# One edge addition instead of two in layer 2, and a blocked layout with one normalization in layer 3

## The chip, the cores and the metric

The kernel runs on one core of a Trainium2 chip, as one launch. The metric is the device time in microseconds of one execution, from the first to the last instruction and the little that lies around them. The numbers are fp32 throughout.

## The reference

Four residual layers follow each other on an image batch of 16 x 64 channels x 128 x 128. Each first normalizes over groups of two channels. Layer 0 multiplies by the image's Gram matrix and a 64 x 64 matrix, layer 1 is a pair of 3 x 3 Scharr-like filters per channel, layer 2 shifts a quarter of the channels one column to the left and a quarter to the right and then has a 3 x 3 convolution with bias, layer 3 has a 3 x 3 convolution, a 1 x 1 convolution and a normalization over the whole batch.

```python
def _gn(v, G=32, eps=1e-5):                       # before every layer
    g = v.reshape(B_, G, C_ // G, H_, W_)
    m = jnp.mean(g, axis=(2, 3, 4), keepdims=True)
    s = jnp.var(g, axis=(2, 3, 4), keepdims=True)
    return ((g - m) / jnp.sqrt(s + eps)).reshape(v.shape)

def _L2_conv_ref(x, W, b):
    def _temporal_shift(x):
        q = x.shape[1] // 4
        left = jnp.concatenate([x[:, :q, :, 1:], jnp.zeros_like(x[:, :q, :, :1])], axis=-1)
        right = jnp.concatenate([jnp.zeros_like(x[:, q:2 * q, :, :1]), x[:, q:2 * q, :, :-1]], axis=-1)
        return jnp.concatenate([left, right, x[:, 2 * q:]], axis=1)
    xs = _temporal_shift(x)
    out = lax.conv_general_dilated(xs, W, window_strides=(1, 1), padding='SAME', ...)
    return out + b[None, :, None, None]

def _L3_conv_ref(x, w_bin, w1x1, b1x1, gamma, beta):
    y = _conv(x, w_bin, [(1, 1), (1, 1)])
    y = _conv(y, w1x1, [(0, 0), (0, 0)]) + b1x1[None, :, None, None]
    mean = jnp.mean(y, axis=(0, 2, 3), keepdims=True)
    var = jnp.var(y, axis=(0, 2, 3), keepdims=True)
    y = (y - mean) * jax.lax.rsqrt(var + EPS)
    y = y * gamma[None, :, None, None] + beta[None, :, None, None]
    y = jnp.where(y >= 0, y, LEAK * y)
    return jnp.clip(y, 0.0, CEIL)

x = x + _L0_conv_ref(_gn(x), L0_conv_conv_w)
x = x + _L1_conv_ref(_gn(x))
x = x + _L2_conv_ref(_gn(x), L2_conv_W, L2_conv_b)
x = x + _L3_conv_ref(_gn(x), L3_conv_w_bin, L3_conv_w1x1, L3_conv_b1x1, L3_conv_gamma, L3_conv_beta)
```

## The kernel before

**Tiling.** Two halves of 64 fill the 128 partitions: for layers 0 and 1 the upper and the lower half of the rows of an image, for layers 2 and 3 two parities of rows. An image is worked in `NS = 8` chunks; a chunk is `R = 8` rows of 128 columns for each partition (`CP = 4` rows of each parity).

**Stages and their order.** Four stages work on different images at the same time: `Gram` (the image's Gram matrix and the small chain of coefficients behind it), `Front` (layers 0 and 1, called the front below), `Layer2` and `Layer3`. The main loop (lines 1055 to 1111) runs over steps, each of four quarters `q`. In each quarter Layer 3 comes first, then Layer 2, then Front, then Gram; they start 35, 25 and 15 steps in, and 8 steps further for every image. So in one step, one chunk of each of three images is worked. All engines' instructions keep the order in which the program issues them (the class `InOrder`); there is no scheduler that moves them. A matmul is issued for the two column halves of the array in turn, from two queues (`held`, `issue`, lines 721 to 741).

**Layer 2.** `load` (line 773) fetches the chunk `i + 2`, `at(i, 1)` normalizes the chunk `i + 1` on ACT in place (line 867), lets POOL compute the `edges` of it (lines 870 to 877: for each of the end columns, 8 rows, a term which the shift of the reference needs there), and POOL clears the end columns of the shifted quarters. A row convolution of three rows is split as in a fast algorithm: one product on the odd rows that two outputs share (`one`), and products on differences of rows (`d2`, made by DVE in `difference`, line 703) that belong to one output row each (`two[:, 0]`, `two[:, 1]`). A twin `qd2` of each difference, with half of it shifted by a column, is written by two DMAs that POOL issues (`twin`, line 808). Products start in `at(i, 2)` and `at(i, 3)`. `one` is evicted to `c` by ACT. One step later, in `at(i, 0)` (lines 838 to 850), DVE adds the edges to the end columns of `two`, side by side in two operations:

```python
e = self.edges.pop(i - 1).rearrange("p t (m n) -> p t n m", n=2)
for side, w in ((0, 0), (1, W - 1)):
    dve.tensor_add(two[:, :, :, w], two[:, :, :, w], e[:, side])
```

and then forms the chunk `x3` = `two` + `c`, with the sums for the next normalization. `x3` has its rows in two blocks, `[2, CP, W]`; ACT squares and sums it (`square`), and SP stores it for the end. When an image is through, `coefficients` (line 308) makes the scale and bias of layer 3 by a chain of small operations on DVE, PE and ACT, and the sums of layer 2's input do the same for the front's next image.

**Layer 3.** `prepare(i + 1)` in `at(i, 1)` (lines 928 to 946) writes the normalized chunk to the tile `v3`, two buffers of `R + 1 = 9` rows, in the order of the image: row 0 is the last of the chunk before, the odd rows 1, 3, 5, 7 are the first block of `x3`, the rows 2, 4, 6, 8 its second. This takes three activations on ACT: of one row, of four rows with a step of two, and of four rows with a step of two. The last chunk of an image needs a fourth, as its last row takes other coefficients. `by_parity` (line 699) gives the even and odd rows as views, `difference` reads even, odd, and the even ones one further (`after`), and `shared` gives the odd ones to the matmuls. `twin` here is two copies on ACT (line 948). The sum `y` = `two` + `c` is stored by SP; its mean and square sums gather over the whole batch.

**The end.** Once all images are through, the batch's coefficients are made (lines 1115 to 1138), and a last pass reads `y` and `x3` back by DMA in 128 parts, has ACT and DVE finish them, and stores the output. The room for prefetched parts comes from tiles that are done (`rest`, line 1033), among them the two `v3` buffers, of which 8 rows are used.

Of the kernel before, what the change touches and what calls it, by code (L numbers as in the profile page):

```python
# [10 lines left out]
F32 = mybir.dt.float32  # L11
# [4 lines left out]
B, C, H, W = 16, 64, 128, 128  # L16
P = 128
# [3 lines left out]
R = 8  # L21
NS = HH // R
EARLY = 3
CP = 4
# [84 lines left out]
def tile_kernel(ctx: ExitStack, tc: tile.TileContext, x, cw_h, w2_t, b2, wbin_t, w1_t, b1, gamma, beta, consts, out):  # L109
    nc = tc.nc  # L110
    pe, dve, act, sp, pool = (InOrder(tc, e) for e in (nc.tensor, nc.vector, nc.scalar, nc.sync, nc.gpsimd))
# [8 lines left out]
    def k(name):  # L120
        return kc[:, AT[name][0]:AT[name][1]]
# [14 lines left out]
    def flat(ap):  # L136
        return ap.rearrange("p j w -> p (j w)")
# [17 lines left out]
    ring = ctx.enter_context(tc.tile_pool(name="ring", bufs=2))  # L155
# [35 lines left out]

    wb = ring.tile([P, (R + 1) * W + 2], F32, tag="v2", name="wb", bufs=3)
    wb = wb[0:C, 0:9 * C].rearrange("p (y x c) -> p y x c", y=3, x=3)
    w1 = ring.tile([P, R + 1, W], F32, tag="v3", name="w1")[0:C, 0, 0:C]

    sp.dma_start(kc[:, 0:P], consts[:, 0:P])
    pool.dma_start(kc[:, P:K_END], consts[:, P:K_END])
# [499 lines left out]


    def by_parity(t):
        v = t[:, 0:R, :].rearrange("p (j s) w -> p s j w", s=2)  # L700
        return v[:, 0], v[:, 1]

    def difference(name, n, t, m=CP):


        even, odd = by_parity(t)
        after = t[:, 1:R + 1, :].rearrange("p (j s) w -> p s j w", s=2)[:, 1]
        dve.tensor_sub(diffs[name][:, n, 0:m, 1:1 + W], (after if n else even)[:, 0:m], odd[:, 0:m])

    def taps(o, p, wts, srcs, pad=0):  # L710
# [37 lines left out]
    def shared(p, wt, t, m=CP):  # L748
        products(p[:, 0:m], [wt], [by_parity(t)[1][:, 0:m]])
# [15 lines left out]
    class Layer2:  # L765
# [65 lines left out]
        def at(self, i, q):  # L831
            b = self.b
            closing = i + 1 == NS
            m = CP - 1 if closing else CP
            if q == 0:
                if i == NS:
                    chains.append(coefficients(self.st, self.done))
                if 1 <= i:
                    two = self.p.pop(i - 1)[0]

                    e = self.edges.pop(i - 1).rearrange("p t (m n) -> p t n m", n=2)
                    for side, w in ((0, 0), (1, W - 1)):
                        dve.tensor_add(two[:, :, :, w], two[:, :, :, w], e[:, side])
                    x3 = ring.tile([P, 2, CP, W], F32, tag="x3", name=f"x3_{b}_{i - 1}", bufs=NS + 2)
                    tiles3[b].append(x3)
                    dve.scalar_tensor_tensor(
                        x3.rearrange("p s j w -> p s (j w)"), two.rearrange("p s j w -> p s (j w)"), 1.0,
                        self.c.unsqueeze(1).to_broadcast([P, 2, CP * W]),
                        op0=ALU.mult, op1=ALU.add, accum_out=self.st[:, 0, i - 1:i],
                    )  # L850
                if 0 <= i < NS:
                    difference("d2", 0, self.v[i], m)
                    self.twin(0)
            if q == 1:
                if i == 0:

                    self.wi = stp.tile([P, 2, 3, P], F32, tag="wi", name=f"wi_{b}", bufs=1)
                    for n, base in ((0, w2[:, 2]), (1, wm)):
                        dve.scalar_tensor_tensor(
                            self.wi[:, n].rearrange("p k o -> p (k o)"), k("I3"), self.co[:, 2:3],  # L860
                            base.rearrange("p k o -> p (k o)"), op0=ALU.mult, op1=ALU.add,
                        )
                if -1 <= i < NS - 1:
                    if i == -1:
                        self.co = coefs2.pop(b)
                    t, f = self.v[i + 1], self.whole.pop(i + 1)
                    act.activation(f, f, AF.Identity, bias=self.co[:, 1:2], scale=self.co[:, 0:1])


                    e = stp.tile([P, 2, R], F32, tag="edges", name=f"edges_{b}_{i + 1}", bufs=3)  # L870
                    for side, at in ((0, 0), (1, W + 1)):
                        for rows, j in ((lo, 1), (hi, 0)):
                            n = at + j * W
                            pool.tensor_scalar_mul(
                                e[rows, side], f[rows, n:n + (R - 1) * W + 1:W], self.co[rows, 3 + side:4 + side]
                            )
                    self.edges[i + 1] = e

                    pool.tensor_scalar_mul(t[:, :, 0], t[:, :, 0], k("keep0"))
                    pool.tensor_scalar_mul(t[:, :, W - 1], t[:, :, W - 1], k("keep1"))  # L880
                if i + 2 < NS:
                    self.load(i + 2)
            if q == 2:
                if 0 <= i < NS:
                    t = self.v[i]
                    one = ps_one.tile([P, CP, W], F32, tag="one", name=f"one2_{b}_{i}")
                    two = ps_two.tile([P, 2, CP, W], F32, tag="two", name=f"two2_{b}_{i}")
                    self.p[i] = two, one
                    shared(one, self.wi[:, 0], t, m)
                    if closing:  # L890
                        small_product(one[:, m, :], w0, t[:, R, :])

                    both = self.wi[:, 1]
                    own(two[:, 1], 1, TO_SLOTS, w2, "d2", m, both)
                    if closing:

                        p = two[:, 1, m:CP]
                        issue([taps(0, p, [both], [t[:, R:R + 1, :]]), taps(1, p, [both], [t[:, R - 1:R, :]])])

                    self.c = ring.tile([P, CP * W], F32, tag="c2", name=f"c2_{b}_{i}", bufs=1)  # L900
                    act.activation(self.c, flat(one), AF.Identity, bias=self.co[:, 5:6])
                if 1 <= i < NS:
                    self.square(i - 1)
                if 1 <= i:
                    self.store(i - 1)
            if q == 3:
                if 0 <= i < NS:
                    t = self.v.pop(i)
                    two, one = self.p[i]
                    both = self.wi[:, 1]  # L910
                    own(two[:, 0], 0, TO_SLOTS, w2, "d2", m, both)
                    if closing:
                        p, srcs = two[:, 0, m:CP], [t[:, R - 2:R - 1, :], t[:, R - 1:R, :]]
                        issue([taps(0, p, [w2[:, 0], both], srcs), taps(1, p, [both, w2[:, 1]], srcs)])
            if q == "last of 0" and i == NS:
                self.square(i - 1)
            if q == "last of 3" and -1 <= i < NS - 1:
                difference("d2", 1, self.v[i + 1], CP if i + 2 < NS else CP - 1)
                self.twin(1)


    class Layer3:
# [4 lines left out]

        def prepare(self, i):
            b, tiles = self.b, tiles3[self.b]
            t = ring.tile([P, R + 1, W], F32, tag="v3", name=f"v3_{b}_{i}")  # L930
            self.v[i] = t

            def norm(dst, src, co):
                act.activation(dst, src, AF.Identity, bias=co[:, 1:2], scale=co[:, 0:1])

            if i == 0:
                self.co, self.edge = coefs3.pop(b)
                norm(t[:, 0, :], tiles[NS - 1][:, 1, CP - 1, :], self.edge["lower"])
            else:
                norm(t[:, 0, :], tiles[i - 1][:, 1, CP - 1, :], self.co)  # L940
            v = t[:, 1:R + 1, :].rearrange("p (n s) w -> p s n w", s=2)
            norm(v[:, 0], tiles[i][:, 0], self.co)
            m = CP if i + 1 < NS else CP - 1
            norm(v[:, 1, 0:m], tiles[i][:, 1, 0:m], self.co)
            if m < CP:
                norm(t[:, R, :], tiles[i][:, 1, m, :], self.edge["upper"])

        def twin(self, n):

# [83 lines left out]
    def rest(pool, tag, shape, bufs, n=None):  # L1033
        for m in range(bufs if n is None else n):
            t = pool.tile([P] + shape, F32, tag=tag, name=f"end_{tag}_{len(room)}", bufs=bufs)
            while len(t.shape) > 2:
                t = t.rearrange("p a b c -> p (a b) c" if len(t.shape) == 4 else "p a b -> p (a b)")
            room.append(t[:, 0:N])
# [16 lines left out]
    for step in range(starts[2][1] - 2, steps):  # L1055
        now[0] = step
        for q in range(4):
            for b in range(B):

                i = step - starts[2][1] - NS * b  # L1060
# [10 lines left out]
            for b in range(1, B):  # L1071
                at, n = pace[b]
# [25 lines left out]
            if step >= last_one and q == 2:  # L1098

                n = 3 if step == last_one else 1 if step < last_one + NS - 2 else 0  # L1100
# [5 lines left out]
        tick()  # L1106
    rest(ring, "x3", [2, CP, W], NS + 2, NS + 2 - 3 - (NS - 3))
    rest(ring, "y", [2, CP, W], 2)
    rest(ring, "v3", [R + 1, W], 2)
    while len(room) > 1:  # L1110
        fetch()

# [17 lines left out]
    e = cpool.tile([P, 1], F32, name="e_bn")  # L1130
# [56 lines left out]
```

## Time and profile before

| | us |
|---|---|
| median of 3 runs | 2742.17 |
| lowest and highest | 2739.24 and 2742.29 |
| the profiled execution, its own time | 2739.81 |
| span of the profiled execution | 2738.0 |
| busy: PE | 2168.3 (79%) |
| busy: DVE | 2190.3 (80%) |
| busy: ACT | 2108.3 (77%) |
| busy: POOL | 851.7 (31%) |
| mean granted clock of PE, whole span | 0.899 |

PE is the matmul engine (PEld its weight loads, which overlap matmuls), DVE the vector engine, ACT the scalar engine, POOL GpSimd, SP the engine that issues most of the DMAs. A group of instructions is given by line, engine, operation, names of the tiles written and read with partitions x elements, and count; then busy time, mean duration in ns, and the idle time of the engine before them with what ended it. All groups have line 73, as every operation goes through the helper there; so one goes by the tiles' names. In the names, buffer numbers are left out: `two<-two,edges` is the edge addition, `v<-x,co` layer 3's normalization, `v<-v,co` layer 2's, `d<-v` a difference, `qd<-d` a twin.

The page has the span in 40 slices of 68 us. The main loop takes about the first 2290 us; PE, DVE and ACT are at 90% or near it from slice 6 to slice 29. Layer 3 of the last image runs alone just before 2290, and from there on the DMAs move 420 GB/s.

### The profile page before, as it was taken

How to read it: one execution, taken by the hardware profiler on the slowest of the kernel's cores; microseconds unless marked ns; L12 is line 12 of the kernel's file. 1: busy time of each engine (PE TensorE's matmuls, PEld its weight loads, DVE VectorE, ACT ScalarE, POOL GpSimd, SP SyncE). 2: the span in 40 equal slices, each digit the busy share in tenths (PEclk: the TensorE clock that was granted, in tenths of full speed). 3: DMA queues.
4: the chain of work that ended last, by engine and by line, in shares of the span. 5: the costliest groups of instructions: out<-in, count | busy, mean ns of one | idle time of the engine just before them, and what ended most of it. 6: DMA issues, size and time to landing. Idle time of an engine off the chain costs nothing. (4 is left out here: it accounts for less than half of the span.)

```text
span 2738.0 us, 45982 instructions
## 1 busy us (share of the span) xinstructions
PE 2168.3 (79%) x14804; PEld 910.8 (33%) x14804; DVE 2190.3 (80%) x3623; ACT 2108.3 (77%) x3177; POOL 851.7 (31%) x1350
## 2 busy tenths in 40 slices
PE   6578899999999999999999999999999993000000
PEld 4234433434343434343434343333334641000000
DVE  4999999999999999999999999999996335333332
ACT  4766889898989898989899989898997677333332
POOL 2044424442434243333343434445444300000000
PEclk8689999999999999999999999999999997555555
DMA  8799878898888888888889787888887868999999
GB/s 209 200 232 235 224 198 238 217 240 220 236 231 234 226 228 226 228 224 234 224 226 239 211 201 201 204 211 207 220 204 187 226 188 308 419 420 420 420 420 385
DMA packets 693600, 685.95 MB, mean 251 GB/s; under 512 B 60096, under 2 KB 580448, under 8 KB 693360
## 3 DMA queue, kind: packets, MB, share of 16 engines
q1 hardware_dynamic: 668208, 613.83, 76.2%
q0 software_dynamic: 25152, 69.18, 10.0%
q8 instruction: 119, 1.95, 0.3%
q14 instruction: 121, 0.99, 0.1%
HBM read 346.23 MB, written 268.44 MB: 224 GB/s over the span
## 5 line engine op out<-in xcount | busy, mean ns | idle before, releaser
L73 PE MATMUL two<-d,w 128*64 128x508 f32 (+2 forms) x2560 | 855.5, 587 | 0.0
L73 PE MATMUL two<-d,wi 128*64 128x508 f32 (+3 forms) x1536 | 576.1, 578 | 0.0
L73 PE MATMUL two<-qd,pk 128*64 128x512 f32 (+1 forms) x1024 | 521.0, 590 | 27.9 <-DMA qd<-d 19.8
L73 POOL DMA_DIRECT2D qd<-d x512 | 270.8, 531 | 862.4 <-DVE d L73 284.5
L73 POOL TENSOR_SCALAR edges<-v,co 64x8 f32<-64x8 f32 x512 | 334.9, 654 | 352.5 <-ACT v L73 183.8
L73 DVE TENSOR_TENSOR d<-v 128x512 f32<-128x512 f32 (+1 forms) x512 | 346.0, 678 | 58.1 <-issue 30.8
L73 PEld LDWEIGHTS two<-d,w 128*64 128x64 f32 x2560 | 273.0, 136 | 325.1 <-issue 282.1
L73 PE MATMUL one<-v,w 128*64 128x508 f32 (+2 forms) x1600 | 364.6, 579 | 0.0
L73 PE MATMUL one<-v,wi 128*64 128x508 f32 (+3 forms) x1536 | 353.3, 591 | 2.5 <-issue 1.7
L73 ACT COPY qd<-d 64x512 f32<-64x512 f32 x512 | 315.5, 616 | 18.2 <-DVE d L73 12.2
L73 DVE SCALAR_TENSOR_TENSOR e<-e 128x1032 f32<-128x1032 f32 (+1 forms) x256 | 313.0, 1223 | 0.0
L73 ACT ACTIVATE xh<-po,co 128x128 f32<-128x128 f32 (+1 forms) x480 | 275.4, 623 | 26.1 <-PE po L73 22.4
L73 PEld LDWEIGHTS two<-d,wi 128*64 128x64 f32 x1536 | 178.8, 136 | 200.6 <-issue 178.8
L73 ACT ACTIVATE v<-x,co 128x512 f32<-128x512 f32 (+2 forms) x368 | 235.0, 705 | 0.0
L73 DVE SCALAR_TENSOR_TENSOR y<-two,c 128x1024 f32<-128x1024 f32 x128 | 156.0, 1219 | 94.6 <-ACT v L73 72.6
L73 POOL TENSOR_SCALAR v<-v,kc 128x9 f32<-128x9 f32 x256 | 217.9, 864 | 11.9
L73 PE MATMUL po<-x,abd 64*64 64x512 f32 (+1 forms) x1024 | 177.7, 640 | 46.5 <-ACT xh L73 43.1
L73 ACT ACTIVATE u<-u 128x1024 f32<-128x1024 f32 x128 | 135.4, 1058 | 75.1 <-DVE u L73 74.7
L73 PEld LDWEIGHTS two<-qd,pk 128*64 128x64 f32 x1024 | 130.8, 135 | 183.1 <-issue 86.4
L73 PEld LDWEIGHTS one<-v,w 128*64 128x64 f32 x1600 | 132.1, 136 | 171.7 <-issue 142.8
L73 DVE SCALAR_TENSOR_TENSOR u<-xh 128x1170 f32<-128x1170 f32 x128 | 175.4, 1370 | 3.8 <-ACT xh L73 3.8
L73 ACT ACTIVATE v<-v,co 128x1154 f32<-128x1154 f32 x128 | 172.1, 1345 | 6.0 <-DMA x_d<-x 3.3
(165 smaller groups left out, 3259.1 us busy)
## 6 DMA issues: line engine op xcount, KB each, us to landing
x<-in_x SPq DMA_DIRECT2D x256, 256.0 KB, 4.6
x_d<-u SPq DMA_DIRECT2D x512, 128.0 KB, 4.0
y_d<-y SPq DMA_DIRECT2D x512, 128.0 KB, 3.9
x_d<-x SPq DMA_DIRECT2D x496, 128.0 KB, 2.7
xr<-in_x SPq DMA_DIRECT2D x120, 512.0 KB, 6.2
qd<-d POOLq DMA_DIRECT2D x256, 130.0 KB, 3.4
qd<-d POOLq DMA_DIRECT2D x256, 129.8 KB, 3.9
v<-x_d SPq DMA_DIRECT2D x448, 72.1 KB, 3.0
```

The costliest lines, as they stand in the source:

```text
L73: return self.tc.keep_in_program_order(call(*args, **kwargs))
```

## The change

Two places are edited, and two sizes follow.

In layer 2, both end columns are added by one operation. The view `two[:, :, :, 0:W:W - 1]` takes columns 0 and 127 of the 8 rows, and `edges` is viewed in the same order, so that one addition of 128 x (8 x 2) elements stands in the place of two of 128 x 8.

In layer 3, the tile `v3` no longer has its rows in the image's order. It has `R + 2 = 10` rows: 0 to 3 are the odd rows, 4 is the last row of the chunk before, 5 to 8 are the even ones that follow, 9 is not used. In this layout both blocks of `x3` go to places that are five rows apart, so that one activation normalizes the whole chunk where all of it takes the same coefficients, in the chunks 0 to 6 of an image. The last chunk has the four operations that it had. `prepare` hands on three views (even, odd, after), which `by_parity` passes through when it gets a tuple; `difference` takes `after` from it.

```diff
     def by_parity(t):
+
+        if isinstance(t, tuple):
+            return t
         v = t[:, 0:R, :].rearrange("p (j s) w -> p s j w", s=2)
-        return v[:, 0], v[:, 1]
+        return v[:, 0], v[:, 1], t[:, 1:R + 1, :].rearrange("p (j s) w -> p s j w", s=2)[:, 1]
 
     def difference(name, n, t, m=CP):
-        even, odd = by_parity(t)
-        after = t[:, 1:R + 1, :].rearrange("p (j s) w -> p s j w", s=2)[:, 1]
+        even, odd, after = by_parity(t)
         dve.tensor_sub(diffs[name][:, n, 0:m, 1:1 + W], (after if n else even)[:, 0:m], odd[:, 0:m])
...
-                    e = self.edges.pop(i - 1).rearrange("p t (m n) -> p t n m", n=2)
-                    for side, w in ((0, 0), (1, W - 1)):
-                        dve.tensor_add(two[:, :, :, w], two[:, :, :, w], e[:, side])
+                    e = self.edges.pop(i - 1).rearrange("p t (m n) -> p n m t", n=2)
+                    ends = two[:, :, :, 0:W:W - 1]
+                    dve.tensor_add(ends, ends, e)
...
         def prepare(self, i):
             b, tiles = self.b, tiles3[self.b]
-            t = ring.tile([P, R + 1, W], F32, tag="v3", name=f"v3_{b}_{i}")
-            self.v[i] = t
+
+            t = ring.tile([P, R + 2, W], F32, tag="v3", name=f"v3_{b}_{i}")
+            self.v[i] = t[:, CP:2 * CP], t[:, 0:CP], t[:, CP + 1:R + 1]
...
             if i == 0:
                 self.co, self.edge = coefs3.pop(b)
-                norm(t[:, 0, :], tiles[NS - 1][:, 1, CP - 1, :], self.edge["lower"])
+                norm(t[:, CP, :], tiles[NS - 1][:, 1, CP - 1, :], self.edge["lower"])
             else:
-                norm(t[:, 0, :], tiles[i - 1][:, 1, CP - 1, :], self.co)
-            v = t[:, 1:R + 1, :].rearrange("p (n s) w -> p s n w", s=2)
-            norm(v[:, 0], tiles[i][:, 0], self.co)
-            m = CP if i + 1 < NS else CP - 1
-            norm(v[:, 1, 0:m], tiles[i][:, 1, 0:m], self.co)
-            if m < CP:
-                norm(t[:, R, :], tiles[i][:, 1, m, :], self.edge["upper"])
+                norm(t[:, CP, :], tiles[i - 1][:, 1, CP - 1, :], self.co)
+            if i + 1 < NS:
+                v = t.rearrange("p (s n) w -> p s n w", s=2)[:, :, 0:CP]
+                norm(v.rearrange("p s n w -> p s (n w)"), tiles[i].rearrange("p s n w -> p s (n w)"), self.co)
+            else:
+                norm(t[:, 0:CP, :], tiles[i][:, 0], self.co)
+                norm(t[:, CP + 1:R, :], tiles[i][:, 1, 0:CP - 1], self.co)
+                norm(t[:, R, :], tiles[i][:, 1, CP - 1, :], self.edge["upper"])
```

The other lines of the diff give `R + 2` rows to `v3` where it holds a weight at the start (`w1`) and where its buffers become room for the last pass. In the built program PE, POOL and SP have the same instructions in the same order with the same waits as before. DVE has 128 instructions fewer, ACT 112.

More of the change, by code (lines that the diff above doesn't have):

```diff
@@ L193, in tile_kernel @@
     wb = wb[0:C, 0:9 * C].rearrange("p (y x c) -> p y x c", y=3, x=3)
-    w1 = ring.tile([P, R + 1, W], F32, tag="v3", name="w1")[0:C, 0, 0:C]
+    w1 = ring.tile([P, R + 2, W], F32, tag="v3", name="w1")[0:C, 0, 0:C]
     sp.dma_start(kc[:, 0:P], consts[:, 0:P])
@@ L1108, in tile_kernel @@
     rest(ring, "y", [2, CP, W], 2)
-    rest(ring, "v3", [R + 1, W], 2)
+    rest(ring, "v3", [R + 2, W], 2)
     while len(room) > 1:
```

## The prediction

> **What bounds the kernel now.** The page was read first. Its busy shares (PE 79%, DVE 80%, ACT 77%) name no bound, and its chain of waits reaches back only to 2232 us, into the last layer-3 chunks and the final pass, where neither edit does much. So the span was cut where its character changes, with the view of busy time by windows (columns: window, length, then busy time of PE, PEld, DVE, ACT, POOL, the granted clock, the DMA share):
>
> ```profile
> 173.00:320.00 147.00, 120.02 (x1046) 55.25 (x1044) 136.78 (x268) 105.24 (x151) 73.01 (x97) 0.93 0.95 243
> 320.00:450.00 130.00, 126.64 (x916) 50.10 (x914) 121.48 (x225) 111.66 (x176) 46.02 (x77) 1.00 0.81 209
> 450.00:1640.00 1190.00, 1178.62 (x8252) 476.25 (x8250) 1132.43 (x1917) 1087.89 (x1706) 445.60 (x739) 1.00 0.86 227
> 1640.00:2012.00 372.00, 364.99 (x1920) 132.14 (x1918) 365.71 (x573) 338.90 (x543) 172.22 (x246) 1.00 0.82 208
> 2012.00:2180.00 168.00, 168.00 (x833) 83.34 (x831) 106.61 (x188) 128.92 (x206) 69.20 (x123) 1.00 0.78 203
> 2180.00:2290.00 110.00, 104.63 (x492) 47.34 (x488) 37.23 (x77) 75.63 (x127) 5.92 (x12) 0.99 0.66 195
> 2290.00:2738.00 448.00, 0.00 (x0) 0.00 (x0) 155.90 (x134) 156.47 (x128) 0.00 (x0) 0.50 1.01 412
> ```
>
> Layer 2's edge additions begin at 177 us and layer 3's normalization at 303. In the long stage (450 to 1640, nine images) PE is idle 1190.00 - 1178.62 = 11.4 us, DVE 57.6, ACT 102: PE is the bound, with two engines close behind. From 1640 to 2012 (three images without a Gram matrix beside them) PE is idle 7.0, DVE 6.3: a tie. From 2012 on the front stage is over, PE has no gap and DVE is free for a third. From 2290 the DMAs are full.
>
> PE can win no more than what it waits. The view of waits for PE alone, for 450 to 1640 and then for 1640 to 2012:
>
> ```profile
> PE two L73 <- ACT qd L73: 5.8, 10, 0.7
> PE two L73 <- DMA qd<-d: 5.2, 9, 2.1
> ...
> PE two L73 <- DMA qd<-d: 3.8, 3, 1.6
> PE one L73 <- issue: 1.7, 1, 1.7
> PE bank L73 <- DVE ad L73: 1.1, 1, 1.1
> PE one L73 <- DMA y_d<-y: 0.4, 1, 0.4
> ```
>
> So PE waits for almost one thing, the shifted twin `qd` of a row difference `d`: copied by ACT for layer 3, by POOL's DMAs for layer 2. The timeline of one image (1220 to 1246) shows three such gaps, all where an image of layer 2 closes, and the DVE and ACT timelines just before show why the twin is late:
>
> ```profile
> 1217.00 1.06 ACT L73 ACTIVATE junk<-x 128x1024 bf16<-128x1024 f32 x1
> 1217.97 0.19 ACT L73 ACTIVATION_READ_ACCUMULATOR junk<-x 128x1 f32 x1
> 1218.18 0.17 DVE L73 TENSOR_REDUCE s<-st 128x2 f32<-128x16 f32 x1 [1.93 <-ACT junk L73]
> 1224.89 0.61 PE L73 MATMUL two<-qd,pk 128*64 128x512 f32 x1 [0.44 <-DMA qd<-d]
> 1232.38 0.64 PE L73 MATMUL two<-qd,pk 128*64 128x512 f32 x1 [0.43 <-ACT qd L73]
> 1241.10 0.61 PE L73 MATMUL two<-qd,pk 128*64 128x512 f32 x1 [0.48 <-DMA qd<-d]
> ```
>
> ACT reaches the last square late, because it has been working without a gap for over 20 us; DVE waits 1.93 us for it, then has more than a step's work in a row, and the differences, twins and matmuls behind come late by what is left.
>
> **What the Trainium skill says.** ScalarE: Activation LUTs, "What ACT_TABLE_LOAD costs", gives an activation with a pointer bias as 280 ns + 0.833 ns an element, 93 ns more for each further pointer operand, and an overlap of 93 ns between neighbours. With pointer bias and scale that is 800 ns for 512 elements and 1226 for 1024; the trace has 807 for `v<-x,co` 128x512 and 1237 for `end_x` 128x1024 with the same two pointers. VectorE: DVE Perf Modes, "The TRN2 errata", prices a DVE operation on PSUM at 120 + elements cycles of 0.96 GHz, 133 ns for 8 elements; the trace has 170 in the mean. The measurement decides for the fixed part; that the fixed part is nearly all of it agrees. TensorE: Matmul & The Clock Gate, "What's actually happening", says that idle windows of about 3.4 us halve PE's clock; the 0.93 in 173 to 320 fits, and 1.00 from 320 on.
>
> **The change part by part.**
>
> ```profile
> L73 DVE TENSOR_TENSOR two<-two,edges 128x8 f32<-128x8 f32 x256 | 43.6, 170 | 18.8 <-PE two L73 14.4
> L73 ACT ACTIVATE v<-x,co 128x512 f32<-128x512 f32 x240 | 182.3, 807 | 0.0
> L73 ACT ACTIVATE end_x<-end_x,sh,sc 128x1024 f32<-128x1024 f32 x39 | 47.9, 1237 | 84.2 <-DMA end_x<-y_d 84.2
> 1102.67 1.51 ACT L73 ACTIVATE v<-x,co 128x512 f32<-128x512 f32 x2
> 1214.01 0.38 DVE L73 TENSOR_TENSOR two<-two,edges 128x8 f32<-128x8 f32 x2
> ```
>
> *Edges.* 256 additions become 128, of 16 elements. Two take 0.38 us together (the second also waits for the first, on DVE's own semaphore). A single one: 170 ns and 8 more elements at 1.04 ns (128x512 at 686 ns against 128x1024 at 1219), about 0.18. Saved: 0.20 us of DVE per chunk, 128 x 0.20 = 25.6 us of work. No row shows three-level operands with an inner step of 127 elements, so the bounds are 0.21 saved and nothing saved (if it costs what two did); I take 0.20, as the elements are few.
>
> *Normalization.* In chunks 0 to 6 of each image two activations of 128x512 become one of 128x1024 into two blocks: 16 x 7 = 112 instructions fewer. The pair lasts 1.51 us, one takes 1.237: 0.27 per chunk, 112 x 0.27 = 30 us of ACT. The last chunk keeps its four operations. Bounds: 0.28 and nothing (if the jump between blocks costs a start); I take 0.27, for other activations here write rows with gaps at no extra cost (1057 ns for `e` 128x1024 in rows of 130, and 1057 for `junk`, written in one run).
>
> *Layout.* The differences and matmuls of layer 3 read as many elements as before, in rows side by side; a row of 128 was already one run, so no change. The tile is one row longer, twice. PE, POOL and SP keep their instructions and order; no wait is added, and nothing waits for half a normalization alone, since the first difference of a chunk needs both halves.
>
> *What reaches the end.* Only work just before a wait of PE counts.
> - 2012 to 2738: nothing. Up to 2180 PE is full. In the last image's layer-3 steps of 7.8 us, `y`, difference, twin and matmul form the circle, and the normalization ends before the difference starts (2254.58 against 2255.41 in one step). After that the DMAs rule.
> - 1640 to 2012: 24 additions give DVE 4.8 us, ACT gains as much. PE's waits of 7.0 are the cap, and the 1.7 and 0.4 there need not go. Taken: 4.0.
> - 450 to 1640: in the mid steps of an image PE is full, and 0.2 us of DVE or 0.27 of ACT turns into idle time there. Only the closing counts: one normalization within ACT's gapless stretch before the last square (0.27), and the edge addition between the second and the third gap (0.20): about 0.5 per image of the 1.3 that PE waits. 9 x 0.5 = 4.5, with a little from other steps 5.0.
> - 320 to 450: PE waits 3.4 us; taken 1.0. 173 to 320: DVE is full in half the steps; 9 additions of 0.20, some of it lost: 1.5.
> Sum: 4.0 + 5.0 + 1.0 + 1.5 = 11.5 us.
>
> **The rivals.**
> (A) PE takes it all: the closing gaps stay, because the layer-2 twins come over DMA (3.4 to 3.9 us to landing) and wait for PE's own earlier reads. For it: half of PE's wait at 450 to 1640 names that DMA. Against: DVE's work stands unbroken ahead of the issue. Only about 2 us of the start remain: 2740.
> (B) All of PE's waits go: 11.4 + 7.0 + 3.4 + 2 = 24 us, 2718. For it: what is taken off DVE and ACT (0.2 and 0.27 a step) is more than PE's wait of 1.3 per image of 8 steps. Against: an early engine cannot run ahead over the mid steps where it waits for PE.
> (C) Slower: earlier DVE work moves POOL's twin issues onto SP's loads and stores. The DMA share is 0.94 in one step of an image (1111.8 to 1126.4) and PE already waits for that landing. The price is one late landing per image: over 13 images it passes the gain from 11.5 / 13 = 0.9 us per image on; at 1.6 us it gives 13 x 1.6 - 11.5 = 9 us more, 2751. Against: neither the bytes nor the order change, and the image's other steps have 0.66 to 0.92.
> (D) The edits save nothing (bounds above): 2742, with (A).
>
> **How the numbers follow.** The profiled execution took 2739.8: a span of 2738.0 and 1.8 around it. 2738.0 - 11.5 + 1.8 = 2728.3. It lies 2.4 below the median of 2742.2, which becomes 2730.7; I say 2730. Its own range is 7 to 17 us of gain. About 0.2%, 5.5 us, is what the measurement can tell from no change. Chances: forecast 0.52, B 0.10 (both faster: 0.62), A with D 0.28 (same), C 0.10 (slower). 2717 takes in B's time; 2744 takes in A, D and the noise above them and leaves out most of C.
>
> **What would show it.** 128 additions `two<-two,edges` of 128x16, each under 0.2 us; 112 activations `v<-x,co` of 128x1024 near 1237 ns; DVE's busy time down by about 22 us by the records (128 x 0.17), ACT's by some 42 (112 x 0.377; records overlap). PE's waits for `qd` from 450 to 1640 near 6 instead of 11.0; the period of a middle image (132.3 us between 979.5 and 1111.8) near 131.8, of a late one (122.1) near 120.8; nothing gained after 2012. It is wrong if the waits for `qd` keep their size (A), vanish (B), or grow under DMA's name (C).

## The result, and the profile after

| | median us | runs | lowest and highest | ratio to before, 95% interval |
|---|---|---|---|---|
| before | 2740.39 | 6 | 2737.01 to 2742.29 | |
| after | 2729.22 | 6 | 2728.83 to 2732.05 | 0.996 (0.995 to 0.997) |

The change gains 11.2 us by the medians. The profiled execution of the changed kernel took 2728.97 us with a span of 2727.2, which is 10.8 below the span before. Both edits do what the diff says. The groups of the changed kernel by form (columns as in the page: count, then busy time, mean ns of one, idle time before them):

```profile
L73 DVE TENSOR_TENSOR two<-two,edges 128x16 f32<-128x16 f32 x128 | 22.3, 174 | 14.0 <-PE two L73 14.0
L73 ACT ACTIVATE v<-x,co 128x1024 f32<-128x1024 f32 x112 | 138.3, 1235 | 0.0
L73 ACT ACTIVATE v<-x,co 128x512 f32<-128x512 f32 x16 | 12.9, 804 | 0.0
```

128 additions of 174 ns stand where 256 of 170 were; 112 activations of 1235 ns stand where 224 of 807 were, and the 16 that are left belong to the last chunks. Neither the columns 127 elements apart nor the jump between the two blocks costs anything that shows.

The busy time by windows of the changed kernel, cut as before (length, busy PE, PEld, DVE, ACT, POOL, clock, DMA share, GB/s):

```profile
173.00:320.00 147.00, 121.17 (x1058) 55.76 (x1056) 138.19 (x264) 108.25 (x154) 75.66 (x99) 0.94 0.96 246
320.00:450.00 130.00, 126.86 (x922) 50.53 (x919) 120.61 (x220) 110.28 (x171) 46.90 (x77) 1.00 0.81 212
450.00:1640.00 1190.00, 1179.06 (x8268) 477.30 (x8264) 1125.19 (x1851) 1075.36 (x1651) 450.72 (x741) 1.00 0.86 227
1640.00:2012.00 372.00, 368.51 (x1943) 133.82 (x1944) 366.15 (x552) 337.50 (x524) 174.43 (x249) 1.00 0.82 212
2012.00:2180.00 168.00, 168.00 (x834) 86.83 (x832) 98.55 (x169) 121.63 (x188) 64.29 (x126) 1.00 0.77 204
```

PE's idle time in the long stage is 10.9 us, where it was 11.4: hardly less. Yet images pass faster. To see this the span is cut at the program's own marks, the start of the first `x<-two,c` of each image, which the DVE timeline gives:

| between these starts | before | after | difference |
|---|---|---|---|
| start of the span to image 0 | 177.2 | 178.5 | +1.3 |
| images 0 and 1 | 263.1 | 260.0 | -3.1 |
| images 2 to 10 | 1189.3 | 1184.8 | -4.5 |
| images 11 to 13 | 372.3 | 368.1 | -4.2 |
| image 14 | 109.7 | 109.5 | -0.2 |
| image 15 to the start of the last `y<-two,c` | 173.9 | 174.1 | +0.2 |
| rest, to the end | 452.5 | 452.2 | -0.3 |

A middle image (4 to 6, 8 and 9 are alike) went from 132.3 to 131.8 us, a late one (12 or 13) from 122.1 to 120.7. These lengths mostly repeat within 0.1, except for single images in which PE waits longer for a DMA; the sum over images 2 to 10 takes those in and repeats within about 0.7 (1189.1 to 1189.4 in three versions that save nothing, 1184.8 and 1185.5 in two that save nearly the same), that over images 11 to 13 within about 0.1. The experiments below are read by these lengths and sums, each from one profiled execution. The first two rows aren't used: in a version that saves no work, images 0 and 1 took 261.7, and in another 266.1.

What PE waits for in the changed kernel, from 450 to 1640 and then from 1640 to 2012 (us in total, times, longest):

```profile
PE two L73 <- ACT qd L73: 6.3, 12, 0.7
PE two L73 <- DMA qd<-d: 4.6, 8, 1.3
...
PE one L73 <- issue: 1.4, 1, 1.4
PE two L73 <- DMA qd<-d: 1.3, 1, 1.3
PE bank L73 <- DVE ad L73: 0.6, 1, 0.6
PE one L73 <- DMA y_d<-y: 0.3, 1, 0.3
```

In the late images the DMA's share fell from 3.8 to 1.3. In the long stage the two waits for `qd` still make 10.9, against 11.0. So the time of the long stage fell by 4.5 and the waits that this view counts by 0.1. That contradiction is what the experiments had to settle.

### The profile page after: what moved, and what is told of

Same layout as the page of the kernel before. It is cut to its first block, busy times and chain, and to the rows that moved or that the text cites. A ratio compares the mean times of both kernels' runs of the same rounds, so it can differ in the third digit from the quotient of the medians.

```text
span 2727.2 us, 45742 instructions
## 1 busy us (share of the span) xinstructions
PE 2162.2 (79%) x14804; PEld 913.7 (34%) x14804; DVE 2170.0 (80%) x3495; ACT 2079.2 (76%) x3065; POOL 852.7 (31%) x1350
## 5 line engine op out<-in xcount | busy, mean ns | idle before, releaser
L73 PEld LDWEIGHTS two<-d,w 128*64 128x64 f32 x2560 | 278.7, 136 | 320.0 <-issue 270.9
L73 ACT ACTIVATE v<-x,co 128x1024 f32<-128x1024 f32 (+3 forms) x256 | 203.8, 847 | 0.0
L73 ACT ACTIVATE c<-one,co 128x512 f32<-128x512 f32 x128 | 86.7, 678 | 127.4 <-PE one L73 124.0
```

What stands on the lines that cost most here:

```text
L73: return self.tc.keep_in_program_order(call(*args, **kwargs))
```

## The experiments

The theory at the start: only the steps in which layer 2 closes an image count, as PE waits for twins there; there 0.20 us of DVE and 0.27 of ACT each shorten the way to a twin, and everywhere else the saved time turns into idle time. The rivals: the time comes from one edit alone, or from the new layout, or from DVE's work as such, so that each 0.2 us of it would come back in every chunk. All of the versions, with the sums by stage from each profile (a ratio is to the kernel before as it ran beside that version, so its median differs a little from the 2740.4 here):

| kernel | median us | ratio to before, 95% interval | images 2 to 10 | images 11 to 13 | middle image | late image |
|---|---|---|---|---|---|---|
| before | 2740.4 | | 1189.3 | 372.3 | 132.3 | 122.1 |
| after | 2729.2 | 0.996 (0.995 to 0.997) | 1184.8 | 368.1 | 131.8 | 120.7 |
| one edge addition alone | 2734.0 | 0.9975 (0.9965 to 0.9986) | 1187.9 | 368.5 | 132.1 | 121.0 |
| layout and normalization alone | 2737.6 | 0.9993 (0.9985 to 1.0002) | 1187.0 | 372.3 | 132.0 | 122.1 |
| layout alone | 2741.1 | 1.0002 (0.9993 to 1.001) | 1189.4 | 372.3 | 132.3 | 122.1 |
| four edge additions | 2742.7 | 1.001 (1.0004 to 1.0017) | 1189.9 | 373.6 | 132.4 | 122.5 |
| edge additions by block | 2740.0 | 0.9994 (0.9986 to 1.0003) | 1189.1 | 372.4 | 132.3 | 122.1 |
| after, last square earlier | 2722.3 | 0.9938 (0.9926 to 0.9951) | 1184.1 | 367.5 | 130.7 | 120.5 |
| after, no edges | 2721.3 | 0.993 (0.9918 to 0.9943) | 1182.9 | 364.7 | 131.5 | 119.9 |
| before, last square earlier | 2730.5 | 0.9966 (0.9952 to 0.998) | 1182.4 | 372.2 | 131.1 | 122.0 |
| after, last chunk in three | 2729.0 | 0.996 (0.9947 to 0.9972) | 1185.5 | 368.0 | 131.8 | 120.7 |

**One part at a time.** The edge addition put into the kernel before, and nothing else:

```diff
-                    e = self.edges.pop(i - 1).rearrange("p t (m n) -> p t n m", n=2)
-                    for side, w in ((0, 0), (1, W - 1)):
-                        dve.tensor_add(two[:, :, :, w], two[:, :, :, w], e[:, side])
+                    e = self.edges.pop(i - 1).rearrange("p t (m n) -> p n m t", n=2)
+                    ends = two[:, :, :, 0:W:W - 1]
+                    dve.tensor_add(ends, ends, e)
```

> Only the edge addition is merged; layer 3 normalizes as before. Theory (the prediction's split): DVE is the bound where no Gram matrix runs and in half of the steps before, so this edit alone gives the 4 us of the late images (period 122.1 to about 120.8), some 2 us over the nine middle images (0.2 each: 132.3 to 132.1) and about 2 us before 450: 8 to 9 us, ratio 0.997. Rival D (all of the gain is DVE's): 11 us and middle images at 131.8. Rival S (all of it is ACT's): no more than 2 us.

Measured: 6.2 us by the medians, not 8 to 9: 3.8 in the late images (the changed kernel: 4.2) and 1.4 in the middle ones, near the 4 and 2 expected there; what lies before them repeats too badly to tell.

The changed kernel with the two additions by column again, so that layout and normalization stand alone (the diff above, in reverse):

> Only layer 3's rows lie in blocks and are normalized at once; both end columns are added apart as before. Theory: 0.27 us of ACT counts once per middle image, ahead of the last square: about 2.5 us over nine images (132.3 to 132.0), nothing in the late images (122.1 stays) and nothing in the end: 2 to 3 us, ratio 0.999. Rival D: 0. Rival S: 9 to 11 us.

Measured: 2.6 us by the medians, which taken alone can't be told from no change (the interval reaches 1.0002). The sums tell more: 2.3 us in the middle images, none in the late ones.

The same without the fused activation, so that only the layout is left:

```diff
-                v = t.rearrange("p (s n) w -> p s n w", s=2)[:, :, 0:CP]
-                norm(v.rearrange("p s n w -> p s (n w)"), tiles[i].rearrange("p s n w -> p s (n w)"), self.co)
+                norm(t[:, 0:CP, :], tiles[i][:, 0], self.co)
+                norm(t[:, CP + 1:R + 1, :], tiles[i][:, 1], self.co)
```

> Layer 3's rows lie in blocks, but each block has its own activation (ACT has as many instructions as before), and the end columns are added apart. Theory: the layout itself costs and gives nothing, within 1.5 us of the kernel before; the durations of d<-v (128x512, 686 ns) and of the matmuls of one<-v stay. Rival L (rows side by side are read faster, or blocks written faster): more than 3 us faster.

Measured: no difference in any stage; the differences `d<-v` of 128x512 take 686 ns in the kernel before and 688 in the changed one. The rival of the layout falls. The two parts alone make 1.4 + 2.3 = 3.7 of the 4.5 us in the middle stage, which is as near as such a sum repeats, and 3.8 of the 4.2 in the late one, where both together give a little more.

**Where the 0.20 us of the edge addition comes from.** The kernel before with each addition cut in two by block, so that there are four of 128x4:

```diff
                     for side, w in ((0, 0), (1, W - 1)):
-                        dve.tensor_add(two[:, :, :, w], two[:, :, :, w], e[:, side])
+                        for n in range(2):
+                            dve.tensor_add(two[:, n, :, w], two[:, n, :, w], e[:, side, n])
```

> The kernel before with the edge addition in four operations of 128x4 instead of two of 128x8: some 0.4 us more of DVE per chunk, the other sign and twice the size of the merge. Theory (DVE carries the gain of the merge): late images 8 x 0.4 = 3.3 us longer each (122.1 to 125.4), the start 3 to 4 us longer, the middle images 0.5 to 2 us longer each: 17 to 30 us in all, ratio 1.006 to 1.011. Rival P (PE is the bound and takes up what DVE loses): under 6 us.

Measured: 2.5 us slower than the kernel before beside it (2740.2), not 17 to 30. The DVE timeline (start, length of the run, group, count), here in the version with four:

```profile
1015.79 0.43 DVE L73 TENSOR_TENSOR two<-two,edges 128x4 f32<-128x4 f32 x4
1016.25 1.22 DVE L73 SCALAR_TENSOR_TENSOR x<-two,c 128x1024 f32<-128x1024 f32 x1
```

and in the changed kernel:

```profile
1209.28 0.17 DVE L73 TENSOR_TENSOR two<-two,edges 128x16 f32<-128x16 f32 x1
1209.49 1.22 DVE L73 SCALAR_TENSOR_TENSOR x<-two,c 128x1024 f32<-128x1024 f32 x1
```

Four additions take 0.46 us to the start of `x`, two took 0.41 (1214.01 to 1214.42 in the kernel before), one takes 0.21. Taken singly, the four start 0, 72, 195 and 274 ns after the first, and `x` at 469. The two of one column lie in different blocks and don't wait for each other: the second starts 72 to 79 ns behind the first. An addition that waits for an earlier one, and `x`, which waits for all, start about 0.20 behind what they wait for. So the price goes by links of the chain: two links before and in the version with four (0.41 and 0.46), one after (0.21). The test thus added only some 0.06 us a chunk and not 0.40. With that dose the sign and the size agree with the theory: 8 chunks of 0.05 to 0.06 are 0.4 to 0.5 us, and the late image is 0.4 longer.

Next, two additions by block instead of by column, meant to have no wait between them:

```diff
-                    e = self.edges.pop(i - 1).rearrange("p t (m n) -> p t n m", n=2)
-                    for side, w in ((0, 0), (1, W - 1)):
-                        dve.tensor_add(two[:, :, :, w], two[:, :, :, w], e[:, side])
+                    e = self.edges.pop(i - 1).rearrange("p t (m n) -> p n m t", n=2)
+                    for n in range(2):
+                        ends = two[:, n, :, 0:W:W - 1]
+                        dve.tensor_add(ends, ends, e[:, n])
```

> The kernel before with two edge additions of 128x(4x2), one for each block of rows, so that neither touches what the other wrote and the second need not wait for the first (two of 128x8 by columns did wait). Theory W (the wait of the second addition for the first is most of the 0.20 us): the pair takes about 0.25 us instead of 0.38, so two thirds of the gain of the merged addition: late images at 121.3 instead of 122.1, 4 us in all. Theory I (it is the number of instructions): no gain, 122.1 stays.

```profile
1016.29 0.38 DVE L73 TENSOR_TENSOR two<-two,edges 128x8 f32<-128x8 f32 x2
1016.70 1.22 DVE L73 SCALAR_TENSOR_TENSOR x<-two,c 128x1024 f32<-128x1024 f32 x1
```

This fence is the DVE timeline of that version: still 0.41 to `x`, and in the built program the second addition still waits for the first on DVE's own semaphore. The condition that should have been tested was not made, so this run settles nothing beyond what it repeats: two linked additions cost 0.41, in whatever order their elements are.

**How much of the edge addition's time the kernel feels.** The changed kernel with the edge term of layer 2 left out altogether: the end columns of the shifted quarters lack it, and DVE has another 0.21 us less in each chunk.

```diff
-                    e = self.edges.pop(i - 1).rearrange("p t (m n) -> p n m t", n=2)
-                    ends = two[:, :, :, 0:W:W - 1]
-                    dve.tensor_add(ends, ends, e)
+                    self.edges.pop(i - 1)
```

> The changed kernel without the edge addition: the end columns of layer 2 lack the term of the shift, and DVE has 0.2 us less per chunk. It asks what bounds the late images now. Theory (DVE and PE are level after the change, as image 13 shows PE without a gap): late images 120.7 to no less than 120.3, middle images by 0.2 at most, under 4 us in all. Rival D (DVE is still the bound): another 1.6 us per late image, 120.7 to 119.1, and 7 us or more in all.

Measured: 5.7 us less span than the changed kernel, in between. A middle image is 0.2 shorter, as the theory has it for an engine that is already early in most steps. A late one is 0.8 shorter and so below the theory's floor of 120.3; that is half of the 8 x 0.21 = 1.7 that would come back if DVE were the bound in each chunk. Image 11, the first of the late ones, gets all of it (126.6 to 124.9).

**Time that no view of waits shows.** A step of PE begins with a run of 12 matmuls `one<-v,wi`, so the PE timeline gives the length of each step, from start to start. The steps of a middle image (image 5, us):

| step | before | one edge addition alone | layout and normalization alone | after | after, last square earlier (below) |
|---|---|---|---|---|---|
| first, just after the image before has closed | 16.46 | 16.26 | 16.46 | 16.26 | 16.23 |
| the next five together | 83.80 | 83.85 | 83.77 | 83.77 | 83.78 |
| the last but one | 15.85 | 15.82 | 15.73 | 15.72 | 15.72 |
| the last | 16.17 | 16.18 | 16.01 | 16.03 | 14.85 |

The five steps in the middle keep their length whatever is saved. The edge addition shortens one step, by all of its 0.20, and the normalization two others, by 0.12 and 0.16. The changed kernel has all three, 0.50 us in an image. Why PE's waits don't tell of it, the last of these steps shows, here in the kernel before:

```profile
963.52 0.59 PE L73 MATMUL two<-d,w 128*64 128x512 f32 x1
963.90 0.64 PE L73 MATMUL two<-qd,pk 128*64 128x512 f32 x1
...
967.39 0.64 PE L73 MATMUL two<-qd,pk 128*64 128x512 f32 x1 [0.70 <-ACT qd L73]
```

and in the changed kernel:

```profile
959.73 0.59 PE L73 MATMUL two<-d,w 128*64 128x512 f32 x1
959.95 0.64 PE L73 MATMUL two<-qd,pk 128*64 128x512 f32 x1
...
963.44 0.64 PE L73 MATMUL two<-qd,pk 128*64 128x512 f32 x1 [0.70 <-ACT qd L73]
```

Here the two column halves of the array work side by side, one with the difference `d`, one with its twin `qd`, and on time both start about 0.01 apart. The first twin starts 0.38 behind the other half before, 0.22 behind it after. That isn't counted as waiting, since the other half has a matmul running. The wait that is counted, for the next twin, has the same 0.70 in both and only comes earlier. So the step is 0.14 us shorter and the view of waits is as before.

A late image shows it more strongly. In the kernel before, with the step after the closing of image 12, which is called the closing step here (from 1880.68 to 1897.62), and some matmuls on differences and twins inside it:

```profile
1865.86 2.77 PE L73 MATMUL one<-v,wi 128*64 128x512 f32 x12
...
1880.68 2.80 PE L73 MATMUL one<-v,wi 128*64 128x512 f32 x12
...
1887.19 0.61 PE L73 MATMUL two<-qd,pk 128*64 128x512 f32 x1 [1.14 <-DMA qd<-d]
...
1891.49 1.02 PE L73 MATMUL two<-d,w 128*64 128x512 f32 x2
1892.18 0.64 PE L73 MATMUL two<-qd,pk 128*64 128x512 f32 x1
...
1897.62 2.79 PE L73 MATMUL one<-v,wi 128*64 128x512 f32 x12
...
1912.47 2.79 PE L73 MATMUL one<-v,wi 128*64 128x512 f32 x12
```

in the changed kernel:

```profile
1872.83 2.80 PE L73 MATMUL one<-v,wi 128*64 128x512 f32 x12
...
1878.01 0.59 PE L73 MATMUL two<-qd,pk 128*64 128x512 f32 x1
1878.03 0.59 PE L73 MATMUL two<-d,wi 128*64 128x508 f32 x1
...
1882.28 1.02 PE L73 MATMUL two<-d,w 128*64 128x512 f32 x2
1882.98 0.64 PE L73 MATMUL two<-qd,pk 128*64 128x512 f32 x1
...
1888.42 2.80 PE L73 MATMUL one<-v,wi 128*64 128x512 f32 x12
```

and without the edge term:

```profile
1868.11 2.80 PE L73 MATMUL one<-v,wi 128*64 128x512 f32 x12
...
1877.57 0.59 PE L73 MATMUL two<-d,w 128*64 128x512 f32 x1
1877.58 0.59 PE L73 MATMUL two<-qd,pk 128*64 128x512 f32 x1
...
1882.96 2.79 PE L73 MATMUL one<-v,wi 128*64 128x512 f32 x12
```

Read start to start, a plain step of PE in a late image is 14.85 us (1897.62 to 1912.47 in the kernel before). The closing step takes 16.94 before, 15.59 after, 14.85 without the edges. Before, two twins are late: that of layer 2, for which PE stands still 1.14 us, and that of layer 3, 0.69 behind the other half. After, the first is on time (1878.01, beside 1878.03) and the second still 0.70 behind. Without the edges both are on time. But the second wait never shows as idle time, because the other half has matmuls running meanwhile. The closing step as a window (columns as above), of the changed kernel:

```profile
1872.83:1888.42 15.59, 15.59 (x77) 5.59 (x73) 15.56 (x20) 13.22 (x22) 9.67 (x13) 1.00 0.89 246
```

and without the edges:

```profile
1868.11:1882.96 14.85, 14.85 (x76) 4.89 (x72) 14.85 (x18) 12.70 (x22) 8.98 (x12) 1.00 0.87 231
```

PE is full in both, and one is 0.74 longer, with the same matmuls (the one more in its window is the first of the next step). The Trainium skill (Perfetto Trace Analysis, "Identifying the Most-Contended Engine") says that the busy share of matmuls doesn't measure how close PE is to its limit; this pair of lines agrees, with 0.74 us as the number. The ACT timeline gives the cause of the 0.70, in the changed kernel:

```profile
1880.64 1.06 ACT L73 ACTIVATE junk<-y 128x1024 bf16<-128x1024 f32 x1
1881.59 0.20 ACT L73 ACTIVATION_READ_ACCUMULATOR junk<-y 128x1 f32 x1
1881.68 2.51 ACT L73 COPY qd<-d 64x512 f32<-64x512 f32 x4
```

A twin is two of these copies, each 2.51 / 4 = 0.63: it is complete at 1881.68 + 1.26 = 1882.94, and its matmul starts at 1882.98, while the other half could start at 1882.28. Without the edges the copies begin 7.98 us into the step instead of 8.85.

Two things limit what this step says of the late stage. The closing steps of the two images before it shrink less, from 16.63 to 16.39 and from 17.38 to 17.19. And in image 11 it isn't the closing alone: four of its later steps are 0.20 to 0.52 shorter, 1.4 us together. This comes from the edge addition (image 11 takes 126.5 with it alone, 128.2 with the normalization alone), and DVE is all but full there, 16.60 of 16.82 us in one of these steps in the kernel before. Through image 12 DVE keeps its saving: the first `x` of image 13 starts 2.20 us ahead of PE's closing step, where it was 0.85, and PE gains in that step.

**The last square earlier.** If the closing step sets the time, then taking the wait of DVE for the last square of an image out of ACT's long row should shorten the middle images more than both edits did. In this version the square of an image's last chunk is put ahead of the front's square `junk<-u` on ACT; nothing else moves. On the changed kernel:

```diff
+    due = []
...
                     self.prepare(i + 1, 1)
+                while due:
+                    due.pop()()
...
                     chains.append(coefficients(self.st, self.done))
+                    due.append(lambda: self.square(NS - 1))
...
-            if q == "last of 0" and i == NS:
-                self.square(i - 1)
+            if q == "last of 0" and i == NS and due:
+                due.pop()()
```

> The changed kernel, with the last square of an image of layer 2 ahead of the front's square in ACT's order, nothing else. Theory (the late last square holds DVE up at the closing, and PE's waits for the twins follow from it): DVE's wait for the sums falls from about 1.9 to 1 us, PE's waits of 1.3 us per middle image go to 0.5, middle images 131.8 to 131.0, late ones 120.7 to 120.3, 6 to 9 us faster than the changed kernel. Rival P (PE's own work and the twins' DMA set the period): within 2 us of the changed kernel.

The ACT and DVE timelines of one image in that version:

```profile
1207.24 1.05 ACT L73 ACTIVATE junk<-x 128x1024 bf16<-128x1024 f32 x1
...
1208.41 1.06 ACT L73 ACTIVATE junk<-u 128x1024 bf16<-128x1024 f32 x1
1208.42 0.17 DVE L73 TENSOR_REDUCE s<-st 128x2 f32<-128x16 f32 x1 [0.89 <-ACT junk L73]
```

DVE waits 0.89 us there, where it waited 1.93 in the kernel before; over the nine images 8.9, against 18.6 in the changed kernel. The best middle images take 130.6 and 130.7, images 7 and 8 take 131.0 and 131.1. Two of the nine, though, take 133.0 and 135.0, and the PE timeline of that version shows why:

```profile
707.45 1.04 PE L73 MATMUL two<-qd,pk 128*64 128x512 f32 x1 [2.20 <-DMA qd<-d]
...
1365.91 0.74 PE L73 MATMUL two<-qd,pk 128*64 128x512 f32 x1 [3.61 <-DMA qd<-d]
```

In these two a twin that comes over DMA is late by 2.20 and 3.61 us. PE's recorded waits in the stage are not down to 0.5 us an image, as expected, but up to 14.3 us in all, every one for that DMA, while the images became shorter. The profiled execution (2726.64) is the slowest of this version's five; whether the others lose less to such landings isn't known, as they left no trace. The median is 2722.33, 6.9 us below the changed kernel and 18 below the kernel before. Its interval and that of the changed kernel just touch at 0.995.

The same edit on the kernel before:

> The kernel before (two edge additions, layer 3's rows in the image's order) with the last square of an image ahead of the front's square. Theory (the closing wait was there before the change, and the change took a part of it by 0.27 us of ACT ahead of the square): middle images 132.3 to 131.2, late ones within 0.4, 6 to 9 us faster than the kernel before. Rival (it pays only once DVE and ACT have been relieved): under 3 us.

Measured: 10.8 us by the medians, not 6 to 9. A middle image takes 131.1, as expected: its last step goes from 16.17 to 15.10. The late images stay as they were: DVE's waits for `junk` before `s` are only 2.1 us in all three of them in the kernel before (2.0 with this edit), so there is nothing to gain. The profiled execution is 9.6 us shorter, 6.9 of it in images 2 to 10; the rest lies before image 2, where executions differ by as much, and isn't explained. PE's waits from 450 to 1640 in this version (us, times, longest) are

```profile
PE two L73 <- DMA qd<-d: 8.3, 10, 2.6
```

and those for ACT's twin are gone.

**The last chunk with three activations.** The fused activation also in an image's last chunk, with the last row written once more by its own coefficients:

```diff
-            if i + 1 < NS:
-                v = t.rearrange("p (s n) w -> p s n w", s=2)[:, :, 0:CP]
-                norm(v.rearrange("p s n w -> p s (n w)"), tiles[i].rearrange("p s n w -> p s (n w)"), self.co)
-            else:
-                norm(t[:, 0:CP, :], tiles[i][:, 0], self.co)
-                norm(t[:, CP + 1:R, :], tiles[i][:, 1, 0:CP - 1], self.co)
+            v = t.rearrange("p (s n) w -> p s n w", s=2)[:, :, 0:CP]
+            norm(v.rearrange("p s n w -> p s (n w)"), tiles[i].rearrange("p s n w -> p s (n w)"), self.co)
+            if i + 1 == NS:
                 norm(t[:, R, :], tiles[i][:, 1, CP - 1, :], self.edge["upper"])
```

> The changed kernel, where the last chunk of an image too has all its rows normalized at once, and its last row is then written again with its own coefficients: three activations instead of four, some 0.25 us less of ACT. It stands behind the last square in ACT's order, where ACT waits for DVE soon after. Theory (only ACT's work ahead of the last square counts): no difference from the changed kernel beyond 1.5 us, middle images at 131.8, late ones at 120.7. Rival (any of ACT's work in the closing counts): middle images at 131.5, 3 us faster.

Measured: no difference. From the start of the first of these activations to the end of the last, ACT needs 1.62 us there instead of 1.79, so it saves 0.17 (less than the 0.25 expected, as neighbouring activations overlap; in the other chunks it is 0.28). This normalization is issued a quarter after the last square of layer 2, and in that place the saving is worth nothing.

## Why the prediction was right, and where it wasn't

*The forecast.* 2730 was predicted, 2729.2 came, and the profiled execution gave 10.8 us for the 11.5 of the sum. The two large terms, 9.0 of it, are right by stage. That the total agrees so closely is in part luck, as the terms before 450 below show.

*The edges.* Taken: 0.20 us of DVE a chunk. Measured: `x` starts 0.21 behind the first addition instead of 0.41. The reason given was two prices of 170 ns; the shown one is a link less in a chain, which is why four additions cost hardly more than two.

*The normalization.* Taken: 1237 ns in the place of 1.51 us. Measured: 1235. DVE's busy time fell by 20.3 us (2190.3 to 2170.0), near the 22 expected. But ACT's fell by 29.1 (2108.3 to 2079.2) and not by some 42: the expectation multiplied single durations, though neighbouring records overlap. The 30 us of the sum itself were right.

*The layout.* Costs nothing, as the version with it alone shows.

*Images 2 to 10.* 5.0 taken, 4.5 measured, and by the mechanism named: the steps in the middle of an image keep their length whatever DVE and ACT save, and the closing part gives the time. The 0.20 and 0.27 taken for an image are 0.20 and 0.28 in the table of steps, the second spread over two steps. The "little from other steps" didn't come.

*Images 11 to 13.* 4.0 taken, 4.2 measured. The "tie" of PE and DVE read there is confirmed in part: without the edges 3.4 us come back of the 24 x 0.21 = 5.0 that DVE then saves. That nearly all of it comes from the edges, and none from the normalization alone, was not foreseen: "ACT gains as much" was counted beside DVE's 4.8 us.

*173 to 450 us.* 2.5 taken in all, 1.8 by the table. Executions differ there by more, so that this agreement shows nothing.

*After 2012.* Nothing taken, and nothing came (-0.2, +0.2, -0.3).

*What was wrong.* "PE can win no more than what it waits", and with it the sign to look for, "PE's waits for `qd` from 450 to 1640 near 6 instead of 11.0". They stayed at 10.9. The image whose gaps it read (1220 to 1246) isn't a typical one either: its gap of 0.44 at 1224.89, for a DMA, is missing in image 5, and the image is 132.7 long. By the prediction's own test ("wrong if the waits for `qd` keep their size") rival A would have won, while the images became shorter by just what was forecast. The view counts a wait only when no matmul is in flight; a twin that is late for one column half, while the other half works, costs time that no view of waits shows. In the late closing step before, the excess over a plain step is 16.94 - 14.85 = 2.09 us, and only 1.14 of it is recorded. What PE is recorded as waiting is therefore no cap: the earlier square and the edits together take 132.3 - 130.7 = 1.6 us off a middle image, more than the 1.3 that it was said to wait, and waits are still recorded there.

*Prices.* The 800, 1226 and 133 ns that the prediction sets beside the trace are estimates, worked out from formulas of the Trainium skill. The 133 come from a row for operations that read PSUM and write SBUF (VectorE: DVE Perf Modes, "The TRN2 errata"), while the edge addition writes PSUM too. So they are at best near its price, and the sum rightly used the measured 170. "1.00 from 320 on", said of the clock, holds up to 2180; the same table has 0.99 and 0.50 after that.

*The rivals.* A (PE takes it all) falls by the time and by the lengths of the images. B (all waits go) didn't come about: the late closing step keeps 0.74 us over a plain one, and the middle images keep their recorded waits. D (no saving) falls by the durations. C (a twin's DMA lands late) isn't in the changed kernel, whose longest such wait from 450 to 1640 is 1.3; but it exists: the version with the earlier square loses 2.3 and 4.3 us to it in two images, against its best ones. Whether this comes from where the issue falls among SP's loads and stores was not tried.

## What to carry to other kernels

Where two instructions share the array by column halves, measure a step from start to start and compare it with a plain step; waits and busy shares miss what is late for one half only. Where one engine isn't full throughout, saved work counts only in the steps that end late, so look for those steps first: there the order of two squares on ACT was worth more in a middle image (1.2 us) than both edits together (0.5). And count dependent links before instructions: joining two small operations that wait for each other saves a link, and splitting one into independent pieces cost little here (0.06 us for two more pieces).

## What the runs showed of the hardware

A small DVE operation on PSUM that waits for the one before starts 0.20 us behind it, an independent one 0.07 us behind (four additions of 128x4, each recorded with 162 ns in the mean). The Trainium skill (VectorE: DVE Perf Modes, "The DRAIN you can't avoid") says that chained operations took the same time with a semaphore after each as with one at the end, but also that a next operation that isn't held starts earlier; for operations this short the runs here show the second, at about a third of the distance, so that a wait between two of them isn't free.

A `two<-two,edges` of 16 elements in pairs 127 elements apart takes 174 ns, one of 8 elements 170: 4 ns more for eight more elements and the operands of three levels together, so that what was open in the prediction has no price that shows. An activation of 128x1024 into two blocks with a row between them takes 1235 ns, one into a single run (`end_x`, same pointer operands) 1237.

A matmul of one column half doesn't always hold up the other half behind it. In the late closing step of the changed kernel the program issues `d,w` and `qd,pk` in turn, but the second `d,w` starts at 1882.71 and the first `qd,pk`, late, at 1882.98.
